# Grouped attention layer: maxima and sums turned on VectorE instead of multiplied on TensorE

## The chip, the cores and the metric

The kernel runs on one core of a Trainium2 chip. The core has a matrix engine (TensorE, "PE" in the profile, with its weight loads as "PEld"), a vector engine (VectorE, "DVE"), a scalar engine (ScalarE, "ACT"), a general engine (GpSimd, "POOL") and a queue that only issues transfers (SyncE, "SP"). The metric is device time in microseconds. Three runs of the kernel before took 3808.76 to 3809.16 us, with a median of 3808.96.

## What is computed

Four cross-attention layers in a row, for 4 sequences of 512 queries of width 256, over one context of 1024 keys of width 512 per sequence, all in 4-byte floats. Layers 0, 2 and 3 are "masked": 16 heads of 64, with a bias on a few key columns. Layer 1 is "grouped": 16 heads of 16, in which four query heads share one key and value head. The change touches layer 1 only:

```python
xn = rmsnorm(x, norm_w)
q = (xn @ wq).reshape(B, T, N_HEADS, HEAD_DIM)          # 16 heads of 16
k = (cond @ wk).reshape(B, S, N_KV_HEADS, HEAD_DIM)     # 4 heads of 16
v = (cond @ wv).reshape(B, S, N_KV_HEADS, HEAD_DIM)
qg = q.reshape(B, T, N_KV_HEADS, n_rep, HEAD_DIM)
scores = jnp.einsum('btgrd,bsgd->bgrts', qg, k) * scale
attn = jax.nn.softmax(scores, axis=-1)
out = jnp.einsum('bgrts,bsgd->btgrd', attn, v).reshape(B, T, N_HEADS * HEAD_DIM)
return residual + out @ wo
```

## The kernel before

**Units and steps.** The work is cut into units of two heads. A masked layer has 8 units per sequence, and so has the grouped layer. Two streams of units, the masked and the grouped one, are laid beside each other by the two strings `MASKED_TURNS` and `GROUPED_TURNS` (line 55): each of 104 positions is a step with a masked unit `g`, a grouped unit `lam`, or both. 72 steps have a masked unit alone, 8 a grouped one alone, 24 have both. The main loop (line 967) writes out the order of every engine's queue by hand, and each queue runs in that order.

**A masked unit in its step.** `scores` (line 642) makes eight tiles of scores, 128 keys by 2 x 512 columns, each with products at L652; ScalarE copies each to SBUF (L662), and VectorE keeps a running maximum over the tiles (L666). The maximum is reduced over the keys (`max_quarters`, L712 to L737), spread by a turn (`max_everywhere`, L744), subtracted (L749); ScalarE takes the exponentials in place (L755), and GpSimd the running sum of them (L794). In the next step the unit, now called `g1`, is multiplied with its values (`attend`, L684) and divided by its sums (`reciprocal_sums`, L804 to L820, and `scale_out`, L829). `project_out` (L840, L862) adds the projection to the state a step later. The rest of the TensorE time, the `fill` list of the main loop, is projections of queries (L548), keys (L472) and values (L514) of units to come.

**A grouped unit.** It takes parts of two steps. In the first, where it is called `coming`, `maxima_pair` (line 602) makes its scores for the first time, in four pairs of tiles spread over the end of the step, and VectorE keeps the running maximum of both heads in `g.mx` (L608). Behind the fourth pair `max_columns` (line 723) reduces it over the keys, so that a maximum per query stands in columns (`g.mcol`). `lower_queries` (line 622) then multiplies those columns, widened to 32, with the identity (L629), which lays each head's maxima along all 32 rows of that head; VectorE takes them from row 16 of each head's queries (L634; `row16` is one in rows 16, 48, 80 and 112 and zero elsewhere, and row 16 of the keys is one). It runs inside the score loop of the next step, behind tile 5, or, where the next step has no masked unit, at the end of the step. In the second step, where the unit is called `lam`, `exponentials_pair` (line 637) makes the scores again, now lowered by the maximum, and ScalarE writes the exponentials (L639). `attend` multiplies them with the values, whose column 16 of every 32 is one, so that row 16 of each head's output is the sum of its exponentials; `keep_even` and `keep_odd` (L694, L698) put the outputs of two units into one tile `o`.

**The sums.** When a pair of units is through (`lam.h == 1`), `sums_grouped` (line 701) multiplies `o` with a selector `sel` (L704), which puts each head's row 16 on all its 32 rows. `normalise_grouped` (line 796) then calls `reciprocal_rows` (line 564): a turn of 32x32 blocks (L570), the reciprocal of one column in 32 (L571), a turn back from a broadcast operand (L572); and multiplies `o` with it (L799). This is the last thing of the step ahead of the next step's scores.

**The banks.** All of PSUM is one tile of eight banks. `Place` (line 95) hands out one bank or an aligned pair, always the one that was returned longest ago in the order of the program (a single bank rather from a pair whose other half is out); `back` returns it. A tile of scores takes a pair, and an engine waits until the last user of its bank is through. The place of the sums product is held from L704 to L799 in the program's order, but on the chip only L570 reads it.

Of the kernel before, what the change touches and what calls it, by code (L numbers as in the profile page):

```python
# [12 lines left out]
ALU = mybir.AluOpType  # L13
# [3 lines left out]
P = 128  # L17
B, S, C = 4, 512, 256
T, CT = 1024, 512
NI = S // P  # L20
NT = T // P
# [54 lines left out]
def kernel(ctx: ExitStack, tc: tile.TileContext, a: dict, out: bass.AP):  # L76
    nc = tc.nc
# [7 lines left out]
    def t_(shape, tag, name, bufs=1, dtype=FP):  # L85
        return sb.tile(shape, dtype, tag=tag, name=name, bufs=bufs)
# [31 lines left out]
    def st_slot(n):  # L118
        return st_all[:, n // (NT + 1), n % (NT + 1), :]
# [4 lines left out]
    ident = t_([P, P], "ident", "ident")  # L124
# [2 lines left out]
    nc.vector.memset(ones, 1.0)  # L127
    eps = t_([P, 1], "eps", "eps")
    nc.vector.memset(eps, EPS)

    sel = t_([P, 4, 32], "sel", "sel")
    nc.vector.tensor_copy(
        sel, ident.rearrange("p (g d) -> p g d", d=32)[:, :, 16:17].to_broadcast([P, 4, 32])
    )


    row16 = t_([P, 2], "row16", "row16")
    nc.vector.reduce_sum(
# [316 lines left out]
    gq = {}  # L455
# [108 lines left out]
    def reciprocal_rows(out_, in_, room):  # L564


        turned = room[:, 0:S]
        short = t_([P, S // 32, 1], "short", f"short{len(turns)}")
        turns.append(0)
        nc.vector.transpose(turned, in_)  # L570
        nc.vector.reciprocal(short, turned.rearrange("p (c r) -> p c r", r=32)[:, :, 0:1])  # L571
        nc.vector.transpose(  # L572
            out_.rearrange("p (c r) -> p c r", r=32), short.to_broadcast([P, S // 32, 32])
        )
# [27 lines left out]
    def maxima_pair(g, i):  # L602

        for odd, w in enumerate(logits_pair(g, i)):
            if i == 0 and odd == 0:
                nc.scalar.copy(g.mx, w.ap)
            else:
                nc.vector.tensor_tensor(g.mx, g.mx, w.ap, ALU.max)  # L608
            w.back()
# [9 lines left out]
                )  # L619
        return ws  # L620

    def lower_queries(g):

        w = Place(1)
        m = w.ap
        for n in range(NI):
            for c in range(4):
                column = NI * (c % 2) + n
                nc.tensor.matmul(  # L629
                    m[32 * c : 32 * (c + 1), n * P : (n + 1) * P],  # L630
                    lhsT=g.mcol[:, column : column + 1].to_broadcast([P, 32]), rhs=ident,
                    start=True, stop=True,
                )
        nc.vector.scalar_tensor_tensor(g.qt, m, row16[:, 1:2], g.qt, ALU.mult, ALU.add)  # L634
        w.back()

    def exponentials_pair(g, i):
        for odd, w in enumerate(logits_pair(g, i)):
            nc.scalar.activation(g.st[2 * i + odd], w.ap, AF.Exp)  # L639
            w.back()  # L640

    def scores(g, within):
        g.st = [st_slot((NT + 1) * g.ring + t) for t in range(NT)]
        g.mx = st_slot((NT + 1) * g.ring + NT)
        g.mx_place = Place()
        for t in range(NT):

            w = Place() if t else g.mx_place
            m = w.ap
            keys = slice(t * P, (t + 1) * P)  # L650
            for j in range(2):
                nc.tensor.matmul(  # L652
                    m[:, j * S : (j + 1) * S], lhsT=g.kt[g.rows[j], keys], rhs=g.qt[g.rows[j], :],
                    start=True, stop=t > 0,
                )
            if t == 0:
                for j in range(2):
                    nc.tensor.matmul(  # L658
                        m[:, j * S : (j + 1) * S], lhsT=aug_k[g.l][g.rows[j], keys],
                        rhs=aug_q[g.rows[j], :], start=False, stop=True,  # L660
                    )
            nc.scalar.copy(g.st[t], m)  # L662
            if t:
                w.back()
                top = g.mx_place.ap
                nc.vector.tensor_tensor(top, top, g.st[t], ALU.max)  # L666
            if t == 5:
                within()

    def place_out(g, width=1):  # L670
        g.place = Place(width)
# [26 lines left out]
        nc.vector.tensor_tensor(half, half, g.po[64:128, :], ALU.add)  # L698
        g.place.back()

    def sums_grouped(g):
        g.place = Place(1)
        g.psum = g.place.ap
        nc.tensor.matmul(  # L704
            g.psum, lhsT=sel.rearrange("p g d -> p (g d)"), rhs=gq[g.b, "o"], start=True, stop=True
        )

# [5 lines left out]
    def max_halves(g, of):  # L716
        quarter = t_([P, 32], "quarter", f"quarter_{g.name}")
        half = t_([64, 32], "half", f"half_{g.name}")
        over_quarter(quarter, of, ALU.max)
        nc.vector.tensor_tensor(half, quarter[0:64, :], quarter[64:128, :], ALU.max)  # L720
        return half

    def max_columns(g):

        half = max_halves(g, g.mx)
        g.mcol = t_([P, 2 * NI], "mcol", f"mcol_{g.name}", bufs=3)
        of = half.rearrange("x (c h) -> x h c", h=4)
        for h in range(4):
            nc.vector.tensor_tensor(
                g.mcol[32 * h : 32 * (h + 1), :], of[0:32, h, :], of[32:64, h, :], ALU.max  # L730
            )

    def max_quarters(g):
        half = max_halves(g, g.mx_place.ap)
        g.every = t_([P, 2 * S // 32, 1], "every", f"every_{g.name}")
        for h in range(4):
            nc.vector.tensor_tensor(  # L737
                g.every[32 * h : 32 * (h + 1), :, 0], half[0:32, :], half[32:64, :], ALU.max
            )
# [53 lines left out]
    def running_sum(g, t):  # L793
        nc.gpsimd.tensor_tensor(g.acc, g.st[0] if t == 1 else g.acc, g.st[t], ALU.add)  # L794

    def normalise_grouped(g, room):
        g.ot = t_([P, S], "ot", f"ot_{g.name}", bufs=3)
        reciprocal_rows(g.ot, g.psum, room)
        nc.vector.tensor_tensor(g.ot, gq[g.b, "o"], g.ot, ALU.mult)  # L799
        g.place.back()  # L800

    def reciprocal_sums(g):

# [98 lines left out]
    def at(n):  # L902
        return steps[n] if 0 <= n < len(steps) else (None, None)

    def masked_at(n):
        return masked[n] if n < len(masked) else None
# [56 lines left out]
    count = 0  # L963
# [3 lines left out]
    for n in range(len(steps) + 2):  # L967
        g, lam = at(n)
        follows, coming = at(n + 1)
# [39 lines left out]
        def behind_exponentials():  # L1009
            pass_events(99.0)  # L1010
            while late:
                late.pop(0)()

        def pair(i):
            if i == 0:
                behind_exponentials()
            maxima_pair(coming, i)
            if i == NT // 2 - 1:
                max_columns(coming)

        if coming:
            share(coming)
# [12 lines left out]

        if g:
            g.now = NT if masked_at(g.n + 1) else 4
            scores(g, lambda: lower_queries(lam) if lam else None)

        ending = n >= len(steps) - 2  # L1040
        if g1 and (g or lam):
# [6 lines left out]
        if lam:  # L1048
            if g1:
                reciprocal_sums(g1)  # L1050
            for i in range(NT // 2):
                if g1:
                    attend(g1, range(2 * i, 2 * i + 2))
                if coming and not g:
                    pair(i)
                exponentials_pair(lam, i)
                if i == 0 and g:
                    g.mx_place.back()
                if not g:
                    if i == 1 and outs:  # L1060
                        project_out(outs.pop(0))()
                    if i == 2 and queries:
                        project_q(queries.pop(0))()
# [78 lines left out]
        for us, w in fill:  # L1142
            while pairs and pairs[0][0] <= now:
                pair(pairs.pop(0)[1])
                now += 1.0
                pairs = [(max(at, now + 1.6), i) for at, i in pairs]
            done = w()
            now += us
            if callable(done):
                pass_events(now)  # L1150
                done()
        while pairs:
            pair(pairs.pop(0)[1])
        behind_exponentials()
        if coming and not follows:
            lower_queries(coming)
        if lam and lam.h == 1:
            sums_grouped(lam)
            normalise_grouped(lam, st_slot((NT + 1) * (count % 2) + NT))
            ready.append(lam)  # L1160
        if g1 and g1 not in ready:
            ready.append(g1)
# [30 lines left out]
```

## Time and profile before

| | |
|---|---|
| median of three runs | 3808.96 us |
| profiled execution | 3809.19 us, its span 3807.4 us |
| TensorE clock granted | 0.997 of full speed |
| ScalarE, L755 exponentials, masked | 768 of 1.054 us |
| VectorE, L749 and L666 | 768 of 1.212 us, 672 of 1.232 us |
| VectorE, L608 maxima, grouped | 224 of 1.220 us |
| GpSimd, L794 running sums | 668 of 2.365 us |

The profile counts time as busy when an instruction of the engine is under way. A product of 4-byte floats stands in the list as two records, so the counts of TensorE rows are twice the number of calls. [...] what a product costs is the distance of starts in the timeline. In a row of groups the figures behind the first bar are busy time in all and mean nanoseconds of one, behind the second the idle time of the engine just before them and what ended it.

### The profile page before, as it was taken

The page shows a single profiled execution, that of the slowest core. Times are in us where ns is not written, and L with a number is a line of the kernel's source. Part 1 is how long each engine was busy: PE and PEld are TensorE (multiplying, and loading weights), DVE is VectorE, ACT ScalarE, POOL GpSimd, SP SyncE. Part 2 cuts the span into 40 slices and gives each one's busy share as a digit, 9 for nine tenths or more (in the row PEclk, how much of TensorE's full clock was granted, in tenths as well). Part 3 has the DMA queues.
Part 4 walks back from the last instruction along what each step waited for, and adds up shares of the span by engine and source line. Part 5 has one row for each costly group of instructions (what it writes and reads, how often), then busy time and mean ns, then how long its engine had stood idle before and what let it go on. Part 6 is the DMA issues. An engine that isn't in the chain of part 4 may idle for free.

```text
span 3807.4 us, 50450 instructions
## 1 busy us (share of the span) xinstructions
PE 3741.1 (98%) x19662; PEld 1879.9 (49%) x19662; DVE 3001.7 (79%) x3928; ACT 2101.8 (55%) x2433; POOL 1624.5 (43%) x749
## 2 busy tenths in 40 slices
PE   8999999999999999999999999999999999999998
PEld 4555444554434555555545444555444355555554
DVE  6887778778877888888887887788787778888887
ACT  4555455555545555555555555555555455555554
POOL 3555113443313555555553333445332155555554
PEclk9999999999999999999999999999999999999999
DMA  2111000010000001101011010100100000000100
GB/s 67 42 31 26 12 24 18 17 33 22 19 11 23 26 26 42 37 26 31 26 25 36 27 27 18 29 26 19 28 20 23 11 25 26 25 26 26 31 24 7
DMA packets 187874, 98.71 MB, mean 26 GB/s; under 512 B 43240, under 2 KB 183528, under 8 KB 187636
## 3 DMA queue, kind: packets, MB, share of 16 engines
q1 hardware_dynamic: 182510, 82.90, 7.9%
q0 software_dynamic: 2560, 8.39, 0.8%
q10 hardware_dynamic: 2566, 4.20, 0.5%
q8 instruction: 155, 2.54, 0.3%
q14 instruction: 83, 0.68, 0.1%
HBM read 89.16 MB, written 2.10 MB: 24 GB/s over the span
## 4 chain that ended last, share of the span: by engine, by line
PE 87%; DVE 8%; ACT 2%; issue 2%; DMA 0%; POOL 0%; DVEq 0%; ACTq 0%; POOLq 0%
PE ps L514 19%; PE ps L684 19%; PE ps L472 17%; PE ps L652 13%; PE ps L616 7%; PE ps L840 5%; PE ps L548 5%; DVE ps L666 4%; ACT st L662 1%; DVE st L749 1%; DVE st L608 1%; PE ps L490 1%; PE ps L658 1%; DVE qt L634 1%; PE ps L704 0%
## 5 line engine op out<-in xcount | busy, mean ns | idle before, releaser
L794 POOL TENSOR_TENSOR st<-st 128x1024 f32<-128x1024 f32 x668 | 1579.7, 2365 | 2059.7 <-ACT st L755 2015.7
L666 DVE TENSOR_TENSOR ps<-ps,st 128x1024 f32<-128x1024 f32 x672 | 828.2, 1232 | 466.3 <-ACT st L662 407.4
L755 ACT ACTIVATE st<-st 128x1024 f32<-128x1024 f32 x768 | 783.2, 1054 | 707.1 <-DVE st L749 695.2
L749 DVE TENSOR_TENSOR st<-st,ps 128x1024 f32<-128x1024 f32 x768 | 885.0, 1212 | 3.3
L684 PE MATMUL ps<-st,v 128*64 128x512 f32 (+1 forms) x4064 | 805.7, 597 | 0.5 <-DVE st L608 0.5
L662 ACT COPY st<-ps 128x1024 f32<-128x1024 f32 x768 | 715.4, 1047 | 101.8 <-PE ps L658 81.4
L514 PEld LDWEIGHTS ps<-wv,ctx 128*128 128x128 f32 x6400 | 729.8, 192 | 73.9 <-issue 63.6
L514 PE MATMUL ps<-wv,ctx 128*128 128x128 f32 x6400 | 742.3, 276 | 0.6 <-ACT st L662 0.6
L652 PE MATMUL ps<-qt,kt 64*128 64x512 f32 x3072 | 708.3, 598 | 1.4 <-ACT qt L554 1.4
L472 PE MATMUL ps<-ctx,wk 128*128 128x512 f32 x1536 | 689.6, 598 | 2.2 <-ACT ctx L384 2.2
L684 PEld LDWEIGHTS ps<-st,v 128*64 128x64 f32 (+1 forms) x4064 | 233.5, 130 | 545.6 <-issue 480.7
L472 PEld LDWEIGHTS ps<-ctx,wk 128*128 128x128 f32 x1536 | 288.1, 191 | 389.1 <-issue 373.2
L652 PEld LDWEIGHTS ps<-qt,kt 64*128 64x128 f32 x3072 | 283.8, 186 | 326.4 <-ACT st L662 146.0
L526 ACT COPY v<-ps 128x512 f32<-128x512 f32 x200 | 117.1, 585 | 497.1 <-PE ps L514 493.2
L608 DVE TENSOR_TENSOR st<-st,ps 128x1024 f32<-128x1024 f32 x224 | 273.3, 1220 | 129.8 <-PE ps L616 61.2
L616 PE MATMUL ps<-qt,kt 32*128 32x512 f32 x2048 | 323.8, 645 | 28.1 <-DVE qt L634 16.3
L639 ACT ACTIVATE st<-ps 128x1024 f32<-128x1024 f32 x256 | 248.4, 1023 | 185.2 <-PE ps L616 156.7
L840 PE MATMUL ps<-ot,wo 128*128 128x512 f32 x448 | 217.4, 611 | 1.4 <-DVE ot L829 0.7
L616 PEld LDWEIGHTS ps<-qt,kt 32*128 32x128 f32 x2048 | 103.4, 186 | 214.1 <-issue 57.1
L548 PE MATMUL ps<-x,wq 128*128 128x512 f32 x384 | 185.6, 606 | 1.8 <-ACT x L356 1.1
L477 ACT COPY kt<-ps 128x512 f32<-128x512 f32 x192 | 109.8, 572 | 77.3 <-PE ps L472 77.0
L840 PEld LDWEIGHTS ps<-ot,wo 128*128 128x128 f32 x448 | 78.5, 189 | 135.2 <-issue 124.2
(143 smaller groups left out, 1633.2 us busy)
## 6 DMA issues: line engine op xcount, KB each, us to landing
wk<-in_L_xattn_Wk_dram SPq DMA_DIRECT2D x96, 256.0 KB
wv<-in_L_xattn_Wv_dram SPq DMA_DIRECT2D x96, 256.0 KB
wq<-in_L_xattn_Wq_dram SPq DMA_DIRECT2D x96, 128.0 KB
wo<-in_L_xattn_Wo_dram SPq DMA_DIRECT2D x96, 128.0 KB
qt<-qt ACTq DMA_DIRECT2D x32, 128.0 KB
xraw<-in_x_dram SPq DMA_DIRECT2D x3, 512.0 KB
out_dram<-out SPq DMA_DIRECT2D x3, 512.0 KB
wq<-in_L_xattn_wq_dram SPq DMA_DIRECT2D x32, 32.0 KB
```

Of the source, the lines that this page charges most:

```text
L472: nc.tensor.matmul(m, lhsT=g.wk[:, k, :], rhs=ctx_t[g.b][:, k, n * 512 : (n + 1) * 512], start=(k == 0), stop=(k == KT - 1),)
L514: nc.tensor.matmul(m[:, t * P : (t + 1) * P], lhsT=ctx_t[g.b][:, k, (4 * n + t) * P : (4 * n + t + 1) * P], rhs=g.wv[:, k, :], start=(k == ...
L548: nc.tensor.matmul(m, lhsT=g.wq[:, k, :], rhs=x[:, k, :], start=(k == 0), stop=(k == KC - 1))
L616: nc.tensor.matmul(ws[odd].ap[:, j * S : (j + 1) * S], lhsT=g.kt[rows, i * P : (i + 1) * P], rhs=g.qt[rows, :], start=True, stop=True,)
L652: nc.tensor.matmul(m[:, j * S : (j + 1) * S], lhsT=g.kt[g.rows[j], keys], rhs=g.qt[g.rows[j], :], start=True, stop=t > 0,)
L662: nc.scalar.copy(g.st[t], m)
L666: nc.vector.tensor_tensor(top, top, g.st[t], ALU.max)
L684: nc.tensor.matmul(g.po[at, :], lhsT=g.v[:, t, rows], rhs=g.st[t][:, j * S : (j + 1) * S], start=(t == first), stop=(t == last),)
L749: nc.vector.tensor_tensor(g.st[t], g.st[t], g.mb, ALU.subtract)
L755: nc.scalar.activation(st, st, AF.Exp)
L794: nc.gpsimd.tensor_tensor(g.acc, g.st[0] if t == 1 else g.acc, g.st[t], ALU.add)
L840: nc.tensor.matmul(m[:, k * S : (k + 1) * S], lhsT=g.wo[:, k * P : (k + 1) * P], rhs=g.ot, start=True, stop=True,)
```

## The change

`sums_grouped`, its selector `sel` and the products at L629 and L704 go. `lower_queries` takes the place of `max_columns` behind the fourth pair of maxima, in every step: VectorE combines the maxima into `every` (four small operations as before, on 16 columns instead of 8), turns `every`, read with each column repeated 32 times, into a bank of PSUM, and lowers the queries from there. The calls of `lower_queries` in the score loop and at the end of the step go. `normalise_grouped` turns `o` itself into a bank of PSUM, takes the reciprocal of column 16 of every 32 (that is row 16 of the outputs), turns it back into the same bank and multiplies from there; it no longer uses the slot in SBUF.

```diff
-    sel = t_([P, 4, 32], "sel", "sel")
-    nc.vector.tensor_copy(
-        sel, ident.rearrange("p (g d) -> p g d", d=32)[:, :, 16:17].to_broadcast([P, 4, 32])
-    )
...
-    def lower_queries(g):
-
-        w = Place(1)
-        m = w.ap
-        for n in range(NI):
-            for c in range(4):
-                column = NI * (c % 2) + n
-                nc.tensor.matmul(
-                    m[32 * c : 32 * (c + 1), n * P : (n + 1) * P],
-                    lhsT=g.mcol[:, column : column + 1].to_broadcast([P, 32]), rhs=ident,
-                    start=True, stop=True,
-                )
-        nc.vector.scalar_tensor_tensor(g.qt, m, row16[:, 1:2], g.qt, ALU.mult, ALU.add)
-        w.back()
...
-    def scores(g, within):
+    def scores(g):
...
-            if t == 5:
-                within()
...
-    def sums_grouped(g):
-        g.place = Place(1)
-        g.psum = g.place.ap
-        nc.tensor.matmul(
-            g.psum, lhsT=sel.rearrange("p g d -> p (g d)"), rhs=gq[g.b, "o"], start=True, stop=True
-        )
...
-    def max_columns(g):
+    def lower_queries(g):
+
 
         half = max_halves(g, g.mx)
-        g.mcol = t_([P, 2 * NI], "mcol", f"mcol_{g.name}", bufs=3)
-        of = half.rearrange("x (c h) -> x h c", h=4)
-        for h in range(4):
+        every = t_([P, S // 32, 1], "every1", f"every1_{g.name}")
+        for c in range(4):
+            cols = slice(c % 2 * S // 32, (c % 2 + 1) * S // 32)
             nc.vector.tensor_tensor(
-                g.mcol[32 * h : 32 * (h + 1), :], of[0:32, h, :], of[32:64, h, :], ALU.max
+                every[32 * c : 32 * (c + 1), :, 0], half[0:32, cols], half[32:64, cols], ALU.max
             )
+        w = Place(1)
+        m = w.ap
+        nc.vector.transpose(
+            m.rearrange("p (b r) -> p b r", r=32), every.to_broadcast([P, S // 32, 32])
+        )
+        nc.vector.scalar_tensor_tensor(g.qt, m, row16[:, 1:2], g.qt, ALU.mult, ALU.add)
+        w.back()
...
-    def normalise_grouped(g, room):
+    def normalise_grouped(g):
+
+        o = gq[g.b, "o"]
+        w = Place(1)
+        m = w.ap
+        short = t_([P, S // 32, 1], "short", f"short_{g.name}")
+        nc.vector.transpose(m, o)
+        nc.vector.reciprocal(short, m.rearrange("p (c r) -> p c r", r=32)[:, :, 16:17])
+        nc.vector.transpose(
+            m.rearrange("p (c r) -> p c r", r=32), short.to_broadcast([P, S // 32, 32])
+        )
         g.ot = t_([P, S], "ot", f"ot_{g.name}", bufs=3)
-        reciprocal_rows(g.ot, g.psum, room)
-        nc.vector.tensor_tensor(g.ot, gq[g.b, "o"], g.ot, ALU.mult)
-        g.place.back()
+        nc.vector.tensor_tensor(g.ot, o, m, ALU.mult)
+        w.back()
...
             if i == NT // 2 - 1:
-                max_columns(coming)
+                lower_queries(coming)
...
-            scores(g, lambda: lower_queries(lam) if lam else None)
+            scores(g)
...
-        if coming and not follows:
-            lower_queries(coming)
         if lam and lam.h == 1:
-            sums_grouped(lam)
-            normalise_grouped(lam, st_slot((NT + 1) * (count % 2) + NT))
+            normalise_grouped(lam)
             ready.append(lam)
```

## The prediction

> **What bounds the kernel now.** I read the page's busy line first, then the list of groups by form for the rows that the change touches, then the waits of those rows, then the timeline of TensorE and VectorE in one typical grouped step.
>
> ```profile
> PE 3741.1 (98%) x19662; PEld 1879.9 (49%) x19662; DVE 3001.7 (79%) x3928; ACT 2101.8 (55%) x2433; POOL 1624.5 (43%) x749
> ...
> L629 PE MATMUL ps<-ident,mcol 128*32 128x128 f32 x1024 | 34.5, 275 | 0.0
> L704 PE MATMUL ps<-o,sel 128*128 128x512 f32 x32 | 16.8, 606 | 3.1 <-DVE o L698 3.1
> L634 DVE SCALAR_TENSOR_TENSOR qt<-ps,row,qt 128x512 f32<-128x512 f32 x32 | 23.9, 748 | 7.5 <-PE ps L629 6.9
> L820 DVE STREAM_TRANSPOSE ot<-short 128x512 f32<-128x512 f32 x93 | 66.1, 711 | 3.2
> L744 DVE STREAM_TRANSPOSE ps<-every 128x1024 f32<-128x1024 f32 x96 | 120.7, 1257 | 12.1 <-ACT st L639 4.5
> ```
>
> TensorE is busy 98% of the span, so a product that goes is worth its pace, as long as no wait takes its place. L629 is the spreading of the maxima (512 products, each in the list twice), L704 the sums (16 products). The last two rows price a turn of 512 columns (0.711 us) and show that a turn may write PSUM at the same pace (1.257 us for 1024 columns).
>
> ```profile
> PE ps L616 <- DVE qt L634: 16.3, 26, 2.1
> DVE st L570 <- PE ps L704: 44.8, 8, 11.2
> ```
>
> These are waits (total us, times, longest). TensorE loses 16.3 us to the lowered queries; VectorE stands 44.8 us behind the sums product, which is free unless it is late afterwards. A typical step, TensorE and then VectorE (start, duration):
>
> ```profile
> 2150.09 1.02 PE L704 MATMUL ps<-o,sel 128*128 128x512 f32 x2
> 2151.04 1.13 PE L652 MATMUL ps<-qt,kt 64*128 64x512 f32 x4
> 2152.00 0.38 PE L658 MATMUL ps<-aug_q,aug_k 64*128 64x512 bf16 x2
> 2152.22 4.46 PE L652 MATMUL ps<-qt,kt 64*128 64x512 f32 x20
> 2156.61 1.08 PE L629 MATMUL ps<-ident,mcol 128*32 128x128 f32 x32
> 2157.61 1.99 PE L652 MATMUL ps<-qt,kt 64*128 64x512 f32 x8
> 2159.53 1.94 PE L684 MATMUL ps<-st,v 128*64 128x512 f32 x8
> 2161.76 1.14 PE L616 MATMUL ps<-qt,kt 32*128 32x512 f32 x8 [0.29 <-DVE qt L634]
> ...
> 2150.65 0.76 DVE L729 TENSOR_TENSOR mcol<-half 32x8 f32<-32x8 f32 x4
> 2151.44 0.72 DVE L570 STREAM_TRANSPOSE st<-ps 128x512 f32<-128x512 f32 x1
> 2152.19 0.25 DVE L571 RECIPROCAL short<-st 128x16 f32<-128x16 f32 x1
> 2152.47 0.71 DVE L572 STREAM_TRANSPOSE ot<-short 128x512 f32<-128x512 f32 x1
> 2153.22 0.69 DVE L799 TENSOR_TENSOR ot<-o,ot 128x512 f32<-128x512 f32 x1
> 2154.38 3.91 DVE L666 TENSOR_TENSOR ps<-ps,st 128x1024 f32<-128x1024 f32 x3 [0.47 <-ACT st L662]
> ```
>
> The reader is to see that L629 stands inside the score products, that L704 opens the step, and that VectorE is busy with the normalisation while TensorE already writes score tiles.
>
> [...] the 512-column product takes 0.691 us with its operand in PSUM (L829) and 0.692 in SBUF (L799). [...] the 16 products of L629 take 1.01 us, not the 16 x 0.23 that the pace of L514 (742.3 us / 3200) would give. [...] a bank that VectorE still holds makes TensorE wait; the trace has such waits (L616 on L814, 0.5 us).
>
> **The change part by part.**
>
> *TensorE.* Per unit of the grouped layer 16 products of L629 go: 1.01 us from the timeline (2156.61 to 2157.61), 32 units. Per pair of units L704 goes: 0.95 us, 16 times. That is 32.3 + 15.2 = 47.5 us. With them can go TensorE's waits on L634 (16.3) and on L698 ahead of L704 (3.1): at most 66.9 us.
>
> *VectorE.* Spreading: four combinations of 32x16 cost what four of 32x8 did (0.165 at L814, 0.163 at L729); a turn into PSUM is new; L634 stays. Added 0.73 us with its gap, 32 times, 23.4 us. The turn from a broadcast operand into PSUM is shown by L744 in double width; bounds 0.69 to 0.73, I take 0.711. Normalisation: turn, reciprocal, turn, product as before; only the places differ. Nothing added; [...] I take 0.
>
> *Places in the queues.* L634 moves from the middle of the next step's maxima (L666) to right behind the step's own last maximum, and nothing in VectorE's queue now waits for TensorE there. Behind it stand the normalisation and the next L666. Where the next step opens 3 to 4 us before L666 can start (3.96 us idle at 2105.21), turn and L634 (1.5 us) are hidden in that hole.
>
> *Banks of PSUM.* This is the term that decides. `Place` hands out the bank returned longest ago, so the pair with the last returned bank comes last: in the score loop that is the fourth tile (t=3). At the end of a step with the pair's second unit, the last return is that of the normalisation. Before, its bank was read by L570 alone, finished at 2152.16, and tile 3 started at 2153.98: no wait. Now the bank holds both turned results until the last product (in L799's place). Work it out in the step above. VectorE is through with the four combinations at 2151.41; lowering ends 1.53 later, 2152.94; the normalisation 2.49 later, 2155.43. TensorE without L704 starts tile 0 at 2150.09 and would start tile 3 at 2153.03. It waits until 2155.45: 2.42 us. It had saved 0.95 + 1.01 + 0.29 = 2.25. Net: 0.2 us lost. Tile 2 draws the pair with the lowering's bank (ready 2152.94, due 2152.15), which is inside that wait.
>
> Now the steps by kind, from the two strings of turns:
> - 13 steps with both streams that follow no normalisation (such as the one at 2101.87): 1.01 + 0.42 of wait, the lowering is through in time (2200.96 against tile 2 at 2203.9). One has 0.79 of wait. Sum 19.0.
> - 8 steps with both streams behind a normalisation: seven like the one above (-0.15), and the one at 599.59, where VectorE is later (602.63 against 599.59): 0.86 + 1.01 + 1.36 saved, wait of 3.8 gained, -0.55. Sum -1.6.
> - 4 masked-only steps behind a normalisation: it now runs in VectorE's idle 10.4 us instead of behind L704. 4 x 0.95 = 3.8.
> - The step at 507: L704 with its wait of 1.42, L629 and 2.06 of wait go (5.4), the fourth tile waits 1.6: 3.5 after ScalarE's copies.
> - Two steps behind grouped-only ones, without a normalisation (near 1150 and 3020): 1.01 + 2.1, less 0.9 for the copies of the last two tiles that now end last: 2 x 2.2.
> - 8 starts of grouped-only steps: L608 and its chain bound them. Five without a normalisation: about 1.0 to 1.2 each, 5.4. Three with it: VectorE's chain through L704 goes (1.13 and 0.43 of wait) and 0.73 comes: 1.0, 0.7, 0.7. Sum 7.8.
>
> Total 19.0 - 1.6 + 3.8 + 3.5 + 4.4 + 7.8 = 36.9 us. The profiled execution took 3809.19 us (span 3807.4 and 1.8 around it); less 36.9 is 3772.3. The median of the runs, 3808.96, stands 0.2 below the profiled one, so 3772.
>
> What would be next: in two successive steps with both streams (2101.87 to 2201.82) VectorE is busy 79.9 of 99.95 us; with 1.5 us more in a stretch some 1.3 shorter it has 17 us left. It has room on average; only the places where TensorE waits for it count.
>
> **Rivals.**
> *No wait at the fourth tile*, because another bank is drawn or VectorE is earlier there: the eight steps give 2.25 or more each, and the step at 507 1 us more. For it: nothing but the rotation puts the wait there. Against: the last returned bank comes fourth by the code. Gain 36.9 + 20 = 57, 3752.
> *VectorE's delay goes on*: behind a normalisation L666 starts 1.1 to 1.5 us later (2155.4 against 2154.38), and if the hole of 0.89 us ahead of L829 does not take that up, the eight steps lose 1.5 each, and the grouped-only starts gain nothing. Gain 36.9 - 12 - 7.8 = 17, 3792. Against: L634 leaves the same chain (0.74).
> *Slower: VectorE becomes the bound of the grouped steps.* The removed products are then worth nothing and the 32 turns show in full: 32 x 0.73 = 23, 3832. It decides from the point where the holes of VectorE in such a step (3.96 ahead of L666, 2.85 ahead of L608) are all waits for its own round trip through ScalarE. Against: the 80% above, and that the first hole waits for score tiles, which TensorE now brings sooner.
>
> **How the numbers follow.** The forecast 0.50 (its own range 3762 to 3783), no wait 0.20 (3745 to 3758), delay going on 0.18 (3783 to 3800), slower 0.10, no change 0.02. Range 3746 to 3793: it leaves out the slower case and part of the third. What a measurement can tell is 0.2%, 7.6 us: faster 0.87, the same 0.03, slower 0.10.
>
> **What would show it.** In the new profile: L629 and L704 gone, TensorE's busy time down by some 50 us; VectorE's up by 23; no TensorE wait on the lowered queries ahead of L616; in the steps behind a normalisation a wait of about 1.5 us or more ahead of the fourth score tile on the normalisation's last product, and none there in the other steps. The prediction is wrong if that wait is absent, or if it is found ahead of the first tiles.

## The result, and the profile after

The changed kernel takes 3789.28 us (median of five runs, 3785.15 to 3790.83) against 3808.76 us before on the same chip (3806.66 to 3809.16): a ratio of 0.9947, 95% interval 0.9933 to 0.9962. It gains 19.5 us; the forecast was 37. The profiled execution took 3790.36 us, with a span of 3788.6. It is one of the longer runs: its mean granted clock is 0.992, where the two runs of 3785 us have 0.995.

Line numbers shift: of before's lines L652, L616, L634, L666, L662, L684, L608 are now L631, L610, L708, L645, L641, L661, L602; the lowering's turn is L705, the normalisation is L780 to L786. First the busy line of the page after, and the two groups that are new:

```profile
PE 3721.2 (98%) x18606; PEld 1859.2 (49%) x18606; DVE 3027.7 (80%) x3959; ACT 2105.2 (56%) x2433; POOL 1624.4 (43%) x749
...
L705 DVE STREAM_TRANSPOSE ps<-every 128x512 f32<-128x512 f32 x32 | 23.3, 727 | 3.3 <-DVE every L700 0.5
L782 DVE STREAM_TRANSPOSE ps<-short 128x512 f32<-128x512 f32 x16 | 11.6, 727 | 0.6
```

VectorE's busy time rose by 26.0 us where 23.4 was forecast; the new turns are 23.3 of it (L705, 0.727 us each). TensorE's fell by 19.9 us only, though the 51.3 us of L629 and L704 are gone and the prediction looked for some 50: the products that stayed were busy longer, much of it in spells of half clock, to which we come below. The list of waits of the kernel after (total us, times, longest) shows what stands where the wait on L634 stood:

```profile
PE ps L631 <- DVE qt L708: 6.5, 8, 1.6
...
PE ps L610 <- DVE quarter L682: 5.8, 3, 2.1
PE ps L631 <- DVE ot L786: 4.9, 9, 1.0
PE ps L610 <- DVE ot L786: 4.3, 3, 1.4
```

TensorE waits for VectorE in four ways: for the lowering and for the normalisation ahead of score tiles (L631), and for the normalisation and for the masked maximum ahead of grouped scores (L610). The step of the prediction, now on TensorE and VectorE (start, duration; idle time before it in brackets):

```profile
2141.32 1.13 PE L631 MATMUL ps<-qt,kt 64*128 64x512 f32 x4
2142.29 0.38 PE L637 MATMUL ps<-aug_q,aug_k 64*128 64x512 bf16 x2
2142.50 1.02 PE L631 MATMUL ps<-qt,kt 64*128 64x512 f32 x4
2144.17 1.98 PE L631 MATMUL ps<-qt,kt 64*128 64x512 f32 x6 [0.64 <-DVE qt L708]
2146.57 4.56 PE L631 MATMUL ps<-qt,kt 64*128 64x512 f32 x18 [0.43 <-DVE ot L786]
2151.06 1.94 PE L661 MATMUL ps<-st,v 128*64 128x512 f32 x8
...
2142.60 0.73 DVE L705 STREAM_TRANSPOSE ps<-every 128x512 f32<-128x512 f32 x1
2143.36 0.75 DVE L708 SCALAR_TENSOR_TENSOR qt<-ps,row,qt 128x512 f32<-128x512 f32 x1
2144.03 0.72 DVE L780 STREAM_TRANSPOSE ps<-o 128x512 f32<-128x512 f32 x1
2144.78 0.26 DVE L781 RECIPROCAL short<-ps 128x16 f32<-128x16 f32 x1
2145.07 0.73 DVE L782 STREAM_TRANSPOSE ps<-short 128x512 f32<-128x512 f32 x1
2145.83 0.69 DVE L786 TENSOR_TENSOR ot<-o,ps 128x512 f32<-128x512 f32 x1
2146.44 1.23 DVE L645 TENSOR_TENSOR ps<-ps,st 128x1024 f32<-128x1024 f32 x1
```

The reader is to see that tile 2 (2144.17) starts as L708 ends its read of the bank, and that the second half of tile 3 (2146.57) starts right behind L786: one bank of its pair is the normalisation's. The bracketed idle times, 1.07 us together, understate the loss, since the ends of products are modelled. By starts, the first product with values (L661) comes 9.74 us behind tile 0; before it was 8.49, and 1.01 of that was L629. So 2.3 us are lost here, at tiles 2 and 3 together.

Where the rest went is told by the granted clock. The first two fences are windows of 20 us (busy time of TensorE, its weight loads, VectorE, ScalarE, GpSimd; then the clock, the transfers' share and GB/s) in the second grouped-only stretch, before and, some 9 us earlier in the span, after; the third is TensorE's timeline there, after:

```profile
1120.00:1140.00 20.00, 18.58 (x138) 6.63 (x134) 16.24 (x22) 9.06 (x11) 0.00 (x0) 1.00 0.00 1
```

```profile
1110.00:1130.00 20.00, 17.89 (x90) 5.68 (x87) 14.55 (x21) 7.67 (x8) 0.00 (x0) 0.83 0.00 1
```

```profile
1120.40 4.91 PE L610 MATMUL ps<-qt,kt 32*128 32x512 f32 x18 [1.42 <-DVE ot L786]
1125.24 3.44 PE L827 MATMUL ps<-ot,wo 128*128 128x512 f32 x4
```

0.83 in 20 us is a spell of 6.8 us at half clock: 1122 to 1124 and 1124 to 1126, windows inside it, each have a granted clock of 0.50. Two output products (L827) take 3.44 us in it, where L840 took 1.98 before. Between 40 and 3760 us the trace of before has two such spells (at 519 and 1161), the trace after has eight: at 469, 521, 603, 1121, 1159, 2026, 2985 and 3019, for 3.4 or 6.8 us each. What they cost is my estimate, half of their length: the two products of L827 are 3.37 us from their start to that of the next, 2.98 of them in the spell, where L840 had 1.92, so 1.45 us are lost. At that rate, and where TensorE has no slack, the spells cost 6.8 us before, 22.2 after. The spells in the last 50 us, behind the last unit's scores, are left out here and below, for every trace has one or two there. So is one at 16 us in the trace after: the first scores don't come later for it.

### The profile page after: what moved, and what is told of

Its sections match the earlier page's. It is cut to its first block, busy times and chain, and to the rows that moved or that the text cites. A ratio compares the mean times of both kernels' runs of the same rounds, so it can differ in the third digit from the quotient of the medians.

```text
span 3788.6 us, 48400 instructions
## 1 busy us (share of the span) xinstructions
PE 3721.2 (98%) x18606; PEld 1859.2 (49%) x18606; DVE 3027.7 (80%) x3959; ACT 2105.2 (56%) x2433; POOL 1624.4 (43%) x749
## 4 chain that ended last, share of the span: by engine, by line
PE 89%; DVE 8%; ACT 1%; issue 1%; POOL 0%; DMA 0%; SPq 0%; DVEq 0%; ACTq 0%; POOLq 0%
PE ps L661 19%; PE ps L508 18%; PE ps L466 17%; PE ps L631 16%; PE ps L610 7%; PE ps L827 5%; PE ps L542 5%; DVE ps L645 2%; DVE st L602 1%; DVE st L727 1%; PE ps L484 1%; DVE quarter L682 1%; ACT st L641 1%; PE ps L637 0%; PE ps L372 0%
## 5 line engine op out<-in xcount | busy, mean ns | idle before, releaser
L645 DVE TENSOR_TENSOR ps<-ps,st 128x1024 f32<-128x1024 f32 x672 | 828.4, 1233 | 483.9 <-ACT st L641 423.4
L727 DVE TENSOR_TENSOR st<-st,ps 128x1024 f32<-128x1024 f32 x768 | 885.4, 1214 | 3.3
L661 PE MATMUL ps<-st,v 128*64 128x512 f32 (+1 forms) x4064 | 805.6, 597 | 0.7 <-DVE st L602 0.7
L641 ACT COPY st<-ps 128x1024 f32<-128x1024 f32 x768 | 714.9, 1046 | 92.2 <-PE ps L637 69.9
L631 PE MATMUL ps<-qt,kt 64*128 64x512 f32 x3072 | 715.8, 599 | 12.8 <-DVE qt L708 6.5
L661 PEld LDWEIGHTS ps<-st,v 128*64 128x64 f32 (+1 forms) x4064 | 233.4, 130 | 546.4 <-issue 464.0
L631 PEld LDWEIGHTS ps<-qt,kt 64*128 64x128 f32 x3072 | 289.1, 186 | 347.7 <-ACT st L641 152.7
L602 DVE TENSOR_TENSOR st<-st,ps 128x1024 f32<-128x1024 f32 x224 | 273.4, 1220 | 131.8 <-PE ps L610 66.2
L610 PE MATMUL ps<-qt,kt 32*128 32x512 f32 x2048 | 334.7, 649 | 20.5 <-DVE st L602 6.2
L618 ACT ACTIVATE st<-ps 128x1024 f32<-128x1024 f32 x256 | 250.0, 1027 | 180.1 <-PE ps L610 151.2
L827 PE MATMUL ps<-ot,wo 128*128 128x512 f32 x448 | 220.9, 620 | 1.9 <-DVE ot L816 0.7
L610 PEld LDWEIGHTS ps<-qt,kt 32*128 32x128 f32 x2048 | 104.5, 186 | 215.4 <-issue 41.8
L827 PEld LDWEIGHTS ps<-ot,wo 128*128 128x128 f32 x448 | 79.9, 192 | 139.4 <-issue 127.7
```

Source lines behind the costliest of these rows:

```text
L610: nc.tensor.matmul(ws[odd].ap[:, j * S : (j + 1) * S], lhsT=g.kt[rows, i * P : (i + 1) * P], rhs=g.qt[rows, :], start=True, stop=True,)
L631: nc.tensor.matmul(m[:, j * S : (j + 1) * S], lhsT=g.kt[g.rows[j], keys], rhs=g.qt[g.rows[j], :], start=True, stop=t > 0,)
L661: nc.tensor.matmul(g.po[at, :], lhsT=g.v[:, t, rows], rhs=g.st[t][:, j * S : (j + 1) * S], start=(t == first), stop=(t == last),)
L727: nc.vector.tensor_tensor(g.st[t], g.st[t], g.mb, ALU.subtract)
L827: nc.tensor.matmul(m[:, k * S : (k + 1) * S], lhsT=g.wo[:, k * P : (k + 1) * P], rhs=g.ot, start=True, stop=True,)
```

## The experiments

All times are medians of several runs beside runs of the kernel before on the same chip (3809.02 us for the first four, 3808.82 for the last four); the intervals are of the ratio.

**The normalisation without a bank.**

```diff
-        w = Place(1)
-        m = w.ap
+        g.ot = t_([P, S], "ot", f"ot_{g.name}", bufs=3)
+        m = g.ot
...
-        w.back()
```

> The normalisation stands at the same place of VectorE's queue, but both turns go to SBUF, so it holds no bank. Theory (the bank held until the last product makes tile 3 of the next scores wait, and the wait also brings half-clock spells of TensorE): the wait of 2.3 us goes in 8 steps (18 us), and of the spells those behind these waits (about 3 of 3.4 us each): 3789 - 18 - 10 = about 3760, mean clock 0.996. Rival (it is VectorE's queue that is late, whatever the memory): 3786 to 3790, the waits ahead of the score tiles stay.

Measured 3779.46 us, ratio 0.9924 [0.9910, 0.9938], clock 0.994. TensorE, and then VectorE's normalisation for comparison:

```profile
2137.39 5.42 PE L631 MATMUL ps<-qt,kt 64*128 64x512 f32 x24 [0.64 <-DVE qt L708]
...
2168.67 1.13 PE L610 MATMUL ps<-qt,kt 32*128 32x512 f32 x4 [0.22 <-DVE st L727]
...
2138.28 0.71 DVE L782 STREAM_TRANSPOSE ot<-short 128x512 f32<-128x512 f32 x1
2139.03 0.69 DVE L785 TENSOR_TENSOR ot<-o,ot 128x512 f32<-128x512 f32 x1
2139.64 1.23 DVE L645 TENSOR_TENSOR ps<-ps,st 128x1024 f32<-128x1024 f32 x1
```

Tiles 2 to 7 now run through while VectorE normalises: the bank made tile 3 wait. The wait for the lowering stays. By starts the tiles gain 1.55 us (L661 now 8.19 us behind tile 0). But the whole step gained only 0.2 to 1.1 us of that: VectorE is late all the same, and TensorE meets it later, at the pair of banks with the spread masked maximum (0.22 us idle on L727). Of the 11.2 us by which the last unit's scores start earlier than in the changed kernel, 6.8 are spells that went, the one at 603 among them. Bank and lateness both count; half of each theory held.

**The normalisation earlier.**

```diff
             late.append(lambda: keep_odd(lam))
+            if lam.h == 1:
+                late.append(lambda: normalise_grouped(lam))
...
-            normalise_grouped(lam)
             ready.append(lam)
```

> The normalisation keeps its bank but runs right behind the sum of the two halves of the outputs, ahead of the maxima of the coming unit, where VectorE stands 2 to 3 us. Theory: no wait on it ahead of the scores, and the maxima of the masked unit start 1.5 us earlier: 3755 to 3762. Rival (VectorE is short of time in these steps, so the 2.5 us show wherever they stand, now as later maxima of the coming unit): 3785 to 3792.

Measured 3774.73 us, 0.9910 [0.9895, 0.9925]. VectorE, ahead of the coming unit's maxima:

```profile
2116.24 0.69 DVE L675 TENSOR_TENSOR o<-o,ps 64x512 f32<-64x512 f32 x1
2116.96 0.73 DVE L780 STREAM_TRANSPOSE ps<-o 128x512 f32<-128x512 f32 x1
2117.72 0.26 DVE L781 RECIPROCAL short<-ps 128x16 f32<-128x16 f32 x1
2118.02 0.73 DVE L782 STREAM_TRANSPOSE ps<-short 128x512 f32<-128x512 f32 x1
2118.78 0.69 DVE L786 TENSOR_TENSOR ot<-o,ps 128x512 f32<-128x512 f32 x1
2119.45 1.22 DVE L602 TENSOR_TENSOR st<-st,ps 128x1024 f32<-128x1024 f32 x1
```

In the changed kernel VectorE stood idle here:

```profile
2125.57 0.69 DVE L675 TENSOR_TENSOR o<-o,ps 64x512 f32<-64x512 f32 x1
2128.78 1.22 DVE L602 TENSOR_TENSOR st<-st,ps 128x1024 f32<-128x1024 f32 x1 [2.52 <-ACT st L600]
```

The normalisation fills that hole, and the steps behind it go from about 0.89 us longer than before to 0.66 us shorter. The time itself lies 12.7 us above the upper end of what was expected: the wait for the lowering at tile 2 stays (0.65 us), and so do the spells in and behind the grouped-only stretches (17.1 us lost).

**Each half of the change alone.** The edits put back the sums product with its selector, or `max_columns` and the products of the lowering.

> Only the lowering of the queries is turned on VectorE; the sums keep their product on TensorE. Theory: 32 x 1.0 us of products and most of the 16 us of waits on the lowered queries go, and no bank is held to the end of a normalisation: 3808.8 - 40 = 3769, within 6. Rival (the lowering at the end of the step is what delays VectorE and costs): 3785 or more.

> Only the sums come from the outputs' own rows; the queries are lowered by products as before. Theory: 16 x 0.95 us go, but in the 8 steps with scores behind a normalisation its bank holds tile 3 up by about 0.9 us, so some 5 to 8 us in all: 3801 to 3804. Rival (the bank costs nothing): 3808.8 - 15 = 3794.

Measured 3782.46 us, 0.9930 [0.9916, 0.9943], and 3799.97 us, 0.9975 [0.9965, 0.9986]. Both lie between their theories, the first nearer to the rival, the second nearer to the theory. What counts is the sum: in the profiled executions the masked units' scores of the last step start 27.9 us earlier with the lowering alone and 7.6 us with the sums alone, 35.5 together, and 18.7 us with both. Each is good alone. Of the 16.8 us that are missing with both, 13.7 are spells: 22.2 us are lost to them with both, against 8.5 and 6.8 with one half (6.8 before). The rest fits the collision at the end of the step, where the lowering pushes the normalisation 1.5 us further back: most steps behind a normalisation take 0.9 to 1.5 us more than the two halves would give. With the normalisation moved it is 35.3.

**The lowering without a bank.** This is on top of the earlier normalisation: `m = g.mx[:, 0:S]` stands in place of the `Place` in `lower_queries`.

> As e2_sums_early, and the spread maxima are turned into the slot of the maxima in SBUF, so that the lowering holds no bank either. Theory: tile 2 of the scores no longer waits 0.65 us for the lowered queries in the 8 steps that followed a normalisation: 3774.7 - 5 = 3769.5. Rival (the wait only moves to the next bank): 3773 to 3776.

Measured 3767.08 us, 0.9889 [0.9873, 0.9904]. The wait at tile 2 is gone from the list, the steps behind a normalisation gain 0.1 to 1.1 us more.

**The clock.** The next edit takes only the wait for the masked maximum (L682) from three steps, also on top of the earlier normalisation:

```diff
-                if i == 0 and g:
+                if i == 0 and g and g1:
                     g.mx_place.back()
...
+            if g and not g1:
+                g.mx_place.back()
```

> As e2_sums_early, but in the three steps behind grouped-only ones the pair of banks with the masked maxima is given back behind the exponentials, so that the third pair of grouped scores doesn't draw it. Theory (a TensorE wait of 1.3 us or more in the grouped steps is followed by a half-clock spell of 3.4 or 6.8 us): the waits of 1.57, 2.1 and 2.1 us go to under 0.9, and the spells at 521, 1146 and 3006 go with them: about 3765, mean clock 0.996. Rival (the spells belong to the stage or come by chance): the spells stay, 3770 to 3773.

Measured 3764.69 us, 0.9886 [0.9871, 0.9901]: 10 us better than without the edit. TensorE's timeline without the edit, its window, and then the same two with it:

```profile
1146.74 3.78 PE L610 MATMUL ps<-qt,kt 32*128 32x512 f32 x12 [2.10 <-DVE quarter L682]
```

```profile
1140.00:1160.00 20.00, 17.90 (x77) 6.23 (x76) 19.13 (x23) 14.26 (x17) 3.30 (x2) 0.83 0.01 2
```

```profile
1136.53 7.30 PE L610 MATMUL ps<-qt,kt 32*128 32x512 f32 x32
1144.54 1.98 PE L542 MATMUL ps<-x,wq 128*128 128x512 f32 x4 [0.71 <-ACT st L618]
```

```profile
1140.00:1160.00 20.00, 19.29 (x97) 8.91 (x96) 17.40 (x22) 15.46 (x18) 10.17 (x5) 1.00 0.08 24
```

With the wait goes the spell, at all three places; the ones behind the other waits stay. The time lost to spells falls from 17.1 to 8.5 us, most of the gain; the 5.8 us of waiting were worth little by their own length, about 1 us by subtraction, for TensorE now waits 0.71 us for ScalarE's exponentials (L618). That the spells did not go by chance is borne out by the other runs: all four have a clock of 0.993 without the edit, and of 0.995 or 0.996 with it; and over the six traces that have this wait in the three steps, 17 of the 18 are followed by a spell. The opposite test was to lengthen a wait:

```diff
+        nc.vector.transpose(
+            m.rearrange("p (b r) -> p b r", r=32), every.to_broadcast([P, S // 32, 32])
+        )
```

> The changed kernel with the turn of the spread maxima done twice. Theory (the waits grow with VectorE's work at the end of the step, and waits of 1.3 us and more bring half-clock spells): in the 8 steps behind a normalisation the wait ahead of tiles 2 and 3 grows by 0.73 us, and spells appear behind most of them, 1.7 to 3.4 us each: 3789 + 8 x 0.73 + 3 + 10 to 20 = 3808 to 3818, mean clock 0.988 or less. Rival (waits and spells have nothing to do with each other): 3789 + 9 = 3798 with as many spells as the changed kernel has, 7 between 400 and 3100 us.

Measured 3799.24 us, 0.9976 [0.9966, 0.9986], clock 0.992 in the profiled run. The steps behind a normalisation became 0.4 to 1.1 us longer. The wait at tile 2 became 1.4 us in most of them, 1.75 and 2.35 in two; three of the eight:

```profile
603.03 1.84 PE L631 MATMUL ps<-qt,kt 64*128 64x512 f32 x2 [2.35 <-DVE qt L711]
...
1044.21 1.98 PE L631 MATMUL ps<-qt,kt 64*128 64x512 f32 x6 [1.42 <-DVE qt L711]
...
2150.07 1.98 PE L631 MATMUL ps<-qt,kt 64*128 64x512 f32 x6 [1.75 <-DVE qt L711]
```

But only the longest is followed by a spell, as the wait at its place is in the changed kernel; seven waits of 1.40 to 1.75 us are not, and the time lost is 22.2 us as in the changed kernel. Time (3798 forecast) and number of spells (seven; the changed kernel has eight) are those of the rival. So a wait of that length is not enough by itself: the theory fell in the steps with both streams, and what stands for it in the grouped-only stretches and the steps after them is the run before this one.

**All that helped, together.**

> e5_early_lower_sbuf and e6_early_mx_later together: 3774.7 - 5 - 10 = about 3760, and mean clock 0.996. Rival (gains of one are taken by the other): 3765 or more.

Measured 3754.30 us (3753.36 to 3754.93), 0.9858 [0.9843, 0.9873], clock 0.996. The gains add up; the 3 us beyond what the two runs gave are about what its trace has less of spells (5.1 us lost, against 8.5 in the run without the three waits). It beats the kernel before by 54.5 us and the changed one, measured beside other runs, by 35.

## Why the prediction was right, and where it was half

The time was inside the range, and in the steps with both streams the changed kernel behaves as the prediction had it; the size was half. That it lies inside is owed to the room that the range left for the second rival (3792): the forecast's own range, 3762 to 3783, missed it, and what brought the time there was in the main not that rival but the clock, for which the prediction had nothing. This much is luck. The score products of the masked units give the account (difference of their starts, after less before, in us; spells at half of their length):

| steps | forecast | measured | of it spells |
|---|---|---|---|
| 13 with both streams, no normalisation ahead (with the L704 at the end of ten) | -28.5 | -31.1 | |
| 6 with both streams, behind a normalisation | +6.9 | +8.8 | +3.4 |
| the three grouped-only stretches, with the 5 steps of both streams next to them | -15.4 | +3.1 | +10.2 |
| a step at 2026 | 0 | +1.5 | +1.7 |
| up to the first scores | 0 | -1.0 | |
| sum | -37.0 | -18.7 | +15.3 |

The forecast column is the prediction's own sum in this cut; in the second row the saved L704 stands one row up.

*The bank at tile 3.* Right in place and size: forecast 2.42 us of wait, 2.3 found, and the edit that takes the bank takes the wait at tile 3. Tile 2's wait was forecast at 0.79 (due 2152.15, ready 2152.94); it shows as 0.64 of idle time.

*VectorE's room.* Right: the earlier normalisation hides in a hole of 2.5 us. The second rival, the delay that goes on, is there as well. In these steps it is hidden behind the bank: only the experiment without the bank shows it, as the 0.5 to 1.4 us that did not come.

*The starts of the grouped-only steps (7.8), the step at 507 (3.5) and the two behind grouped-only ones (2.2 each).* This is the step that failed. I took the end of the wait on L634 as the gain, less ScalarE's copies. What came in its place, in the steps next to the grouped-only ones, is the wait for the masked maximum: with the queries ready, TensorE runs into the third pair of grouped scores, which draws the banks of the running maximum, and those are read last by L682:

```profile
519.68 2.87 PE L610 MATMUL ps<-qt,kt 32*128 32x512 f32 x12 [1.57 <-DVE quarter L682]
```

There are three, of 1.57, 2.10 and 2.10 us, as long as the old waits of 2.06. In three starts behind a normalisation the fourth pair of banks waits for L786, 1.42 us each, where the sum had gains of 1.0 and 0.7. The bank named there, the last returned one as at tile 3, is not what costs at these starts. In the run whose normalisation holds no bank TensorE stops at the same three starts, for 1.88, 1.99 and 1.99 us, now for the grouped maxima that stand behind the normalisation in VectorE's queue:

```profile
1116.45 2.41 PE L610 MATMUL ps<-qt,kt 32*128 32x512 f32 x12 [1.99 <-DVE st L602]
```

So here it is the second rival's delay in VectorE's queue that TensorE waits for, with the bank or without. The row misses its forecast by 18.5 us, of which 10.2 are spells. The other 8.3 no run splits between the two kinds of wait: the one that takes the three waits on L682 away gains about 1 us besides its spells, and none takes VectorE's delay at the starts away by itself.

*The clock.* The sum had no term for it. "TensorE is busy 98% of the span, so a product that goes is worth its pace, as long as no wait takes its place" priced a wait at its own length. In this case waits of 1.4 us and more in and behind the grouped-only stretches come with half-clock spells more often than not (32 of the 36 for L682 and for L786, in six traces each), and the trace of before had the sign: its two spells follow the two waits of 2.06 us at 516 and 1157, the first of which is

```profile
517.87 1.86 PE L616 MATMUL ps<-qt,kt 32*128 32x512 f32 x10 [2.06 <-DVE qt L634]
```

With 15.3 of 18.3 us the clock is the larger part of the error.

*Chance.* Whether one given wait is followed by a spell is in part luck. All spells of a trace start on one grid, which means that their starts lie whole multiples of 3.413 us apart, within 0.01 us; and where on that grid a wait begins differs from trace to trace. Two waits that stand in many traces, with the time from the last line of the grid to their start:

| wait of TensorE | a spell follows | no spell follows |
|---|---|---|
| 1.31 us near 2026, in all ten traces | 1.78 to 1.92 us (5 traces) | 0.16 to 1.10 and 2.84 us (5 traces) |
| 1.42 us for the normalisation at the three starts, in six traces | 0.23 to 2.23 us (15 waits) | 2.91 to 2.94 us (3 waits) |

So the spell at 2026, which the kernel before lacks behind a wait as long, is such a chance.

What stays open: why the waits of 1.40 to 1.75 us in the steps with both streams bring no spell (two of the seven begin at 0.29 and 1.86 us of the grid, so the place alone does not decide), nor the third wait of 2.07 us before (at 3034, 2.47 us behind a line), nor five of 1.42 to 1.53 us ahead of a sums product in the stretches (one before, four with the lowering alone), nor any of the forty waits of 1.73 us, four in every trace, ahead of a product in steps with a masked unit alone. That TensorE's other work around the wait decides (products with 32 rows in the stretches) may be, but no run took that apart.

## What to carry to other kernels

When work goes from a busy engine to one with room, look first at what the new work holds while it runs: a rotation that hands out the bank returned longest ago comes round to the last holder's bank within a few tiles, and the tile that draws it waits for that holder. Follow the rotation through every kind of step, not just the commonest. Two edits that each gain can meet in one place, here the end of the step, and a hole earlier in the same queue may be worth more than either. Where a profile has dips of the granted clock, price a TensorE wait together with them, as a range: the same wait may or may not bring one (of the 18 waits of 1.42 us for L786, 15 had a spell behind them and 3 had none).

## What the runs showed of the hardware

The spells at half clock (0.50 granted) last 3.41, 6.83 or 10.24 us, multiples of 3.41, in every trace here, save those that the end of the run cuts short; their starts lie on a grid of the same 3.413 us. In and behind the grouped-only stretches, where TensorE was busy about 18 of 20 us, 17 of 18 waits for L682 and 15 of 18 for L786 were followed by such a drop; in the changed kernel these are six waits of 1.42 to 2.10 us, each with a drop within 4 us of its start. In the run without the three waits for L682 the three drops behind them were gone. So in this case a wait well below the 3.41 us of the shortest spell can be followed by one, and is not always. What lowers the clock was not shown.

A turn of 128x512 from a broadcast operand took 0.727 us into PSUM (L782) against 0.711 into SBUF (L572 before), 16 ns more. A product of two tensors took 0.687 us with an operand in PSUM (L786) and 0.692 with both in SBUF (L799 before).
